# Values and keys in seven products each: keys' first product second, their fourth in front of the seventh, and VectorE's additions for the values ahead of the statistics

## The chip, the core and the metric

The kernel runs on one core of one Trainium2 chip. The metric is the device time of one execution in microseconds (us). The engines of the core are TensorE (PE; PEld is its loading of weights), VectorE (DVE), ScalarE (ACT), GpSimd (POOL) and SyncE (SP, which here only issues DMAs). A measurement of this kernel can tell a difference from none at about 0.2%, that is 4.7 us.

## The reference

Sixteen graphs of 1024 nodes with 256 features go through two layers. Everything is float32.

```python
# layer 0
h = relu(layernorm(x))
c = mean(h over features)                       # one number per node
A = 2 * abs(abs(sigmoid(c[None] - c[:, None]) - 0.5) - 0.5)
g = relu((h.T @ (adj * A)) * para)              # queries, [features, nodes]
k, v = split(h @ kv_w)                          # keys and values, 4 heads of 64
x = x + softmax(q @ k.T * scale) @ v            # attention over the 1024 nodes
# layer 1
h = relu(layernorm(x))
agg = A_hat @ h                                 # A_hat from adj, the same for all graphs
z = agg @ W1.T + b1;  z = relu(batchnorm(z));  z = z @ W2.T + b2
x = x + batchnorm(z)
```

Both batch norms go over all graphs, so there is a first long stage (layer 0, and layer 1 up to `z`) and a second stage that starts when all `z` are known.

## The kernel before

**The loop over graphs.** In the first stage the graphs `b` follow each other. In one pass TensorE does the attention of graph `b` (`attention`), then the queries, values and keys of graph `b + 1` (`graph_seven`), then layer 1 of graph `b` (`linear1`, `linear1_seven`). `graph_seven` runs in 14 passes. In 13 of them `linear1` follows it at once; in the last one (`last` is true) the attention of graph 15 follows, and layer 1 of graph 14 comes later. The order on every engine is written out by hand: inside `tc.manual_schedule` each engine executes in the order of the Python calls. Waits between engines are put in by the framework, from the tiles that instructions read and write.

**Seven products.** A matrix product of 2 by 2 blocks is done with seven block products in place of eight. The class `Seven` does it for the values (`V`, `turned`, so that nodes lie on partitions) and for the keys (`K`). Product 1 is written to one PSUM bank, `x`. ScalarE copies it out (`copy`, L728); then product 6 is added into the same bank, which is copied out again; then product 5, and product 3. Products 2, 7 and 4 have banks of their own, and VectorE adds them onto what was copied (`add`, L731). So a product that is added into `x` must wait until ScalarE has copied what stands there. One product is 8 matmul records of 128 columns for the values (L718) and 2 of 512 for the keys (L713).

**PSUM.** There are three buffers with the tag "s" (two banks each), one with "o" and one with "t". Values' `x` and fourth product and keys' `x` and seventh product take "s"; values' seventh and keys' fourth take "o", one after the other; both second products take "t". The two running sums of the queries, `gps`, hold two "s" buffers before that, and the first two tiles that come after (aggregation in `linear1`, or scores in the last pass) take the buffers of values' fourth product and keys' `x`.

**What stands around it on the other engines.** ScalarE copies the last sum of the queries (L656). VectorE makes sums of parts of `h` for the seven products (L663 to L667), finishes the queries (L657 to L670, L740), adds the attention's second half to `x` (`add1`, L938), and then takes the layer norm of this `x` (`norm`, with the class `Norm`) in two halves of four chunks. For each half: `stats` (L253 and L255) on VectorE, `invert` with the variance on VectorE (L259) and the power on GpSimd (`rstd`, L260), `shifts` on VectorE (L266, which waits for GpSimd), and `relu` on ScalarE (L281), one instruction a chunk, which writes `f_h_b`. The aggregation's first product (`f_aps`, L1027) reads `f_h_b` as weights, chunk by chunk, first the four chunks of the first half, then the second half's.

**SP.** The DMA queue of SP holds here, in order: `leave`, the store of `x` (L1279); `arrive`, the load of the `x` of a later graph into the same buffer (L191, 1 MB), which must wait until the last ReLU has read that buffer; two loads `f_t` (L998) and the load `f_w1s` (L1116). VectorE takes statistics of the arrived `x` (`f_st_a`, L253), GpSimd its power (L260), VectorE its shift (L266, behind the addition L1076 on its engine), and ScalarE its ReLU (`f_h_a`, eight chunks). Behind these on ScalarE stands the copy L1079 of the aggregation's running sum, into which the last product of the aggregation (`s4` by `resident(1, 1)`) is then added.

Of the kernel before, what the change touches and what calls it, by code (L numbers as in the profile page):

```python
# [29 lines left out]
def fast_path(  # L30
# [24 lines left out]
    NC = N // P  # L55
# [120 lines left out]
    with ExitStack() as stage:  # L176
# [332 lines left out]
        def graph_seven(b, left, norm, load_more, last):  # L509
# [224 lines left out]
            K = Seven("k", 0, lambda i, j: kT[:, i, ts(j, 512)], False)  # L734
            V.product(1)
            V.copy(0, 0)
            V.product(2)
            V.add(0, 0, 2)
            for d in range(CC):
# [1 line left out]
            V.product(7)  # L741
            V.product(6)
            V.copy(1, 0)
            K.product(1)
            K.copy(0, 0)
            add1()
            leave(b - 1)
            arrive(b + 1)
            load_more(2, 3)
            norm.stats(0, 4)  # L750
            norm.invert(0, 4)
            K.product(2)
            V.product(5)
            V.copy(1, 1)
            V.add(1, 0, 7)
            V.add(1, 1, 7)
            norm.shifts(0, 4)
            if last:
                K.add(0, 0, 2)
            norm.stats(4, NC)  # L760
            norm.invert(4, NC)
            K.product(6)
            K.copy(1, 0)
            V.product(4)
            V.add(1, 0, 4)
            V.product(3)
            V.copy(0, 1)
            todo = [lambda d=d: relu_queries(d) for d in range(CC)]
# [6 lines left out]
                relu_queries(1)  # L775
            else:
                norm.relu(0, 4, False)
            K.product(7)
            norm.shifts(4, NC)
            if not last:  # L780
                K.add(0, 0, 2)
            K.product(4)
            K.product(3)
            K.copy(0, 1)
            if not last:
# [596 lines left out]
        with tc.manual_schedule(engines={ENG.PE, ENG.Activation, ENG.DVE, ENG.Pool, ENG.SP}):  # L1382
# [3 lines left out]
            norm = Norm(xs[0], "a0", sums_of[0])  # L1386
# [69 lines left out]
            for b in range(B):  # L1456
# [25 lines left out]
                norm = Norm(xr[b], f"b{b}")  # L1482
# [17 lines left out]
                if b + 1 < B:  # L1500
                    more_loads = {}

                    def load_more(k0, k1):
                        if 0 < b < B - 2:
                            more_loads.update(load_thirds(b, k0, k1))

                    if b == 0:
                        qkv = graph(b + 1, between)
                        todo = []
                    else:  # L1510
                        qkv, todo = graph_seven(b + 1, left, norm, load_more, b + 2 == B)
                        thirds = more_loads
                    if b == 0:
                        for step in scale[4:]:
                            step()
                        thirds = make_thirds(b)
# [945 lines left out]
```

## Time and profile before

| | |
|---|---|
| Time, median of 4 runs | 2369.65 us (2369.29 to 2370.03) |
| The profiled execution | 2371.92 us, of which the span of its instructions is 2370.1 us |
| Granted TensorE clock, mean | 0.996 |
| Busy: TensorE, VectorE, ScalarE, GpSimd | 98%, 84%, 60%, 19% |
| From one pass to the next | about 129.2 us |
| Values and keys of one pass, up to the aggregation | 12.5 us |

A row of the timeline tells: start in us, duration in us, engine, line of the kernel, operation, what it writes from what it reads, shape, count of merged instructions; in brackets the engine's idle time ahead of it and what ended it. Matmul records overlap in the pipeline, so the distance of two starts says more than a duration. A weight load normally starts when the matmul before its own starts; its engine's "idle" in between costs nothing.

### The profile page before, as it was taken

The page shows a single profiled execution, that of the slowest core. Times are in us where ns is not written, and L with a number is a line of the kernel's source. Part 1 is how long each engine was busy: PE and PEld are TensorE (multiplying, and loading weights), DVE is VectorE, ACT ScalarE, POOL GpSimd, SP SyncE. Part 2 cuts the span into 40 slices and gives each one's busy share as a digit, 9 for nine tenths or more (in the row PEclk, how much of TensorE's full clock was granted, in tenths as well). Part 3 has the DMA queues.
Part 4 walks back from the last instruction along what each step waited for, and adds up shares of the span by engine and source line. Part 5 has one row for each costly group of instructions (what it writes and reads, how often), then busy time and mean ns, then how long its engine had stood idle before and what let it go on. Part 6 is the DMA issues. An engine that isn't in the chain of part 4 may idle for free.

```text
span 2370.1 us, 25709 instructions
## 1 busy us (share of the span) xinstructions
PE 2328.4 (98%) x8258; PEld 1034.0 (44%) x8258; DVE 1986.2 (84%) x2923; ACT 1417.4 (60%) x2057; POOL 441.9 (19%) x565
## 2 busy tenths in 40 slices
PE   8999999999999999999999999999999999999995
PEld 4444444434343434444343434344444434444444
DVE  6788989897989889897989798988989898757766
ACT  6846556574837465665657384746556575346654
POOL 2041212122221112221212221221212121100000
PEclk9999999999999999999999999999999999999998
DMA  5043343523342434334343324253353521355569
GB/s 187 18 137 104 133 142 116 158 109 116 118 142 78 169 98 155 121 126 150 109 132 132 126 81 159 89 178 98 133 142 116 158 73 54 130 213 179 175 235 375
DMA packets 167264, 323.78 MB, mean 137 GB/s; under 512 B 33616, under 2 KB 100688, under 8 KB 167120
## 3 DMA queue, kind: packets, MB, share of 16 engines
q1 hardware_dynamic: 143696, 266.44, 32.7%
q0 software_dynamic: 18816, 38.83, 6.0%
q10 hardware_dynamic: 4608, 16.78, 1.8%
q8 instruction: 67, 1.10, 0.2%
q14 instruction: 77, 0.63, 0.1%
HBM read 202.38 MB, written 100.72 MB: 128 GB/s over the span
## 4 chain that ended last, share of the span: by engine, by line
PE 93%; DMA 2%; DVE 2%; POOL 1%; issue 1%; ACT 0%; SPq 0%; DVEq 0%; ACTq 0%; POOLq 0%
PE f_s L810 19%; PE f_o L862 19%; PE f_aps L1027 16%; PE f_gps L571 8%; PE f_gpsx L571 6%; PE f_zps L1134 6%; PE f_zx L1684 4%; PE f_zm L1684 3%; PE f_vpsx L718 2%; PE f_kpsx L713 2%; PE f_vps L718 1%; PE f_kps L713 1%; PE f_gps L413 1%; DMA f_z<-fx 1%; PE f_vps L459 1%
## 5 line engine op out<-in xcount | busy, mean ns | idle before, releaser
L818 ACT ACTIVATE f_p<-f_s 128x1024 f32<-128x1024 f32 x512 | 477.0, 1044 | 60.7 <-PE f_s L810 60.6
L810 PE MATMUL f_s<-f_qT,f_kT 64*128 64x512 f32 x2048 | 457.0, 596 | 0.4 <-DVE f_v L731 0.4
L862 PE MATMUL f_o<-f_p,f_v 128*64 128x512 f32 x2048 | 453.6, 595 | 0.0
L810 PEld LDWEIGHTS f_s<-f_qT,f_kT 64*128 64x128 f32 x2048 | 191.1, 185 | 263.8 <-issue 116.9
L862 PEld LDWEIGHTS f_o<-f_p,f_v 128*64 128x64 f32 x2048 | 141.4, 137 | 304.3 <-issue 265.6
L366 POOL TENSOR_TENSOR f_w<-f_w,f_adj 128x1024 f32<-128x1024 f32 x56 | 132.5, 2366 | 701.5 <-ACT f_w L365 528.7
L930 POOL DMA_DIRECT2D f_att<-f_oT x256 | 136.7, 541 | 381.5 <-DVE f_oT L913 375.1
L833 DVE TENSOR_TENSOR f_acc<-f_acc,f_p 128x1024 f32<-128x1024 f32 x128 | 155.9, 1218 | 4.6 <-ACT f_p L818 4.6
L833 DVE TENSOR_TENSOR f_sums<-f_sums,f_p 128x1024 f32<-128x1024 f32 x128 | 155.8, 1217 | 0.0
L353 ACT ACTIVATE f_w<-f_row,f_col 128x1024 f32<-128x1024 f32 x127 | 147.5, 1161 | 7.2 <-DMA f_row<-frow 5.2
L356 ACT ACTIVATE f_w<-f_w 128x1024 f32<-128x1024 f32 x127 | 134.4, 1058 | 4.0
L1027 PE MATMUL f_aps<-f_ahatT,f_hs 128*128 128x512 f32 x256 | 115.1, 592 | 0.0
L1027 PE MATMUL f_aps<-f_ahatT,f_h_b 128*128 128x512 f32 x256 | 113.7, 597 | 0.3 <-DVE f_v L731 0.2
L365 ACT ACTIVATE f_w<-f_w,f_now 128x1024 f32<-128x1024 f32 x56 | 64.4, 1149 | 82.5 <-DVE f_now L363 82.5
L1027 PE MATMUL f_aps<-f_t,f_hs 128*128 128x512 f32 x256 | 112.5, 592 | 0.0
L571 PE MATMUL f_gps<-f_w,f_h_a 128*128 128x512 f32 x224 | 109.9, 592 | 0.0
L824 DVE TENSOR_TENSOR f_acc<-f_p,f_p 128x1024 f32<-128x1024 f32 x64 | 78.0, 1218 | 32.3 <-ACT f_p L818 32.3
L281 ACT ACTIVATE f_h_a<-f_x,f_shift_a,f_rstd_a 128x256 f32<-128x256 f32 x126 | 73.8, 587 | 38.2 <-DVE f_shift_a L266 38.2
L830 DVE TENSOR_TENSOR f_sums<-f_p,f_p 128x1024 f32<-128x1024 f32 x64 | 78.1, 1221 | 21.0 <-ACT f_p L818 21.0
L370 DVE SCALAR_TENSOR_TENSOR f_w<-f_w,f_adj 128x1024 f32<-128x1024 f32 x71 | 88.0, 1258 | 7.7 <-ACT f_w L356 7.6
L1157 ACT ACTIVATE f_z<-f_zps,f_b 128x512 f32<-128x512 f32 x60 | 38.0, 684 | 75.2 <-PE f_zps L1134 75.2
L846 DVE STREAM_TRANSPOSE f_sums<-f_acc 128x1024 f32<-128x1024 f32 x64 | 79.7, 1246 | 1.7
(298 smaller groups left out, 3964.9 us busy)
## 6 DMA issues: line engine op xcount, KB each, us to landing
f_t<-ft SPq DMA_DIRECT2D x84, 512.0 KB, 9.8
fz<-f_z SPq DMA_DIRECT2D x64, 512.0 KB, 9.6
f_x<-in_x_dram SPq DMA_DIRECT2D x31, 1024.0 KB, 6.0
f_zb<-fz SPq DMA_DIRECT2D x42, 512.0 KB, 4.3
fx<-f_x SPq DMA_DIRECT2D x16, 1024.0 KB, 4.4
fgs<-f_gs POOLq DMA_DIRECT2D x28, 512.0 KB, 3.0
fhT<-f_hQ POOLq DMA_DIRECT2D x112, 128.0 KB, 3.2
f_hT<-fhT SPq DMA_DIRECT2D x28, 512.0 KB, 6.2
```

The costliest lines, as they stand in the source:

```text
L353: nc.scalar.activation(w, rows[b], AF.Abs, bias=cols[b][:, c : c + 1], scale=0.5 / C)
L356: nc.scalar.activation(w, w, AF.Tanh)
L366: nc.gpsimd.tensor_mul(w, w, adj_t[c])
L571: nc.tensor.matmul(ps, left, right, start=fresh and n == 0, stop=(n == PAIRS - 1), skip_group_check=more,)
L810: nc.tensor.matmul(ps[:, e, :], kT[rows_e, pair, ts(m, P)], qT[rows_e, pair, ts(g, 512)], start=True, stop=True,)
L818: nc.scalar.activation(p, ps, AF.Exp)
L833: nc.vector.tensor_add(to, to, p)
L862: nc.tensor.matmul(o_of[s][e * HD : (e + 1) * HD, :], v[:, m, ts(2 * pair + e, HD)], p[:, e, :], start=(m == 0), stop=(m == NC - 1),)
L930: queue.dma_start(t[ts(j, 32), :, a].rearrange("r h c i -> r h (c i)"), oT[ts(a, 32), :, j].rearrange("r h c i -> r h (c i)"),)
L1027: nc.tensor.matmul(ps, left[:, m, :], right(m), start=not more and m == 0, stop=(m == KH - 1), skip_group_check=more,)
L1134: nc.tensor.matmul(ps[i], left[:, ts(i, P)], right, start=not more, stop=True, skip_group_check=more,)
L1684: nc.tensor.matmul(ps, left[:, m, :], right[:, m, :], start=start and m == 0, stop=(m == 1), skip_group_check=not start,)
```

## The change

No instruction is added or taken away. On TensorE two products move. Keys' first product moves from the fifth place to the second, directly behind values' first; keys' fourth moves ahead of keys' seventh. On VectorE the two additions of values' seventh product (`V.add(1, 0, 7)`, `V.add(1, 1, 7)`) now stand ahead of the first half's statistics, and the addition of values' fourth product ahead of the first half's shift and the second half's statistics, where it stood behind these. ScalarE, GpSimd and SP keep their order.

On TensorE the order was V1 V2 V7 V6 K1 K2 V5 K6 V4 V3 K5 K7 K4 K3 and becomes V1 K1 V2 V7 V6 K2 V5 K6 V4 V3 K5 K4 K7 K3 (V and K for values and keys, with the number of the product).

```diff
             V.product(1)
             V.copy(0, 0)
+            K.product(1)
             V.product(2)
             V.add(0, 0, 2)
             for d in range(CC):
                 nc.vector.tensor_mul(qT[:, d, :], both(d), qT[:, d, :])
             V.product(7)
             V.product(6)
             V.copy(1, 0)
-            K.product(1)
             K.copy(0, 0)
             add1()
             leave(b - 1)
             arrive(b + 1)
             load_more(2, 3)
-            norm.stats(0, 4)
-            norm.invert(0, 4)
             K.product(2)
             V.product(5)
             V.copy(1, 1)
             V.add(1, 0, 7)
             V.add(1, 1, 7)
-            norm.shifts(0, 4)
+            norm.stats(0, 4)
+            norm.invert(0, 4)
             if last:
                 K.add(0, 0, 2)
-            norm.stats(4, NC)
-            norm.invert(4, NC)
             K.product(6)
             K.copy(1, 0)
             V.product(4)
             V.add(1, 0, 4)
+            norm.shifts(0, 4)
+            norm.stats(4, NC)
+            norm.invert(4, NC)
             V.product(3)
             V.copy(0, 1)
...
-            K.product(7)
+            K.product(4)
             norm.shifts(4, NC)
             if not last:
                 K.add(0, 0, 2)
-            K.product(4)
+            K.product(7)
             K.product(3)
             K.copy(0, 1)
```

## The prediction

> **What bounds the kernel.** I read the page first (engine shares, chain), then the timeline of one pass of `graph_seven`, TensorE alone and then all engines, then the wait lists.
>
> ```profile
> PE 2328.4 (98%) x8258; PEld 1034.0 (44%) x8258; DVE 1986.2 (84%) x2923; ACT 1417.4 (60%) x2057; POOL 441.9 (19%) x565
> PE 93%; DMA 2%; DVE 2%; POOL 1%; issue 1%; ACT 0%; SPq 0%; DVEq 0%; ACTq 0%; POOLq 0%
> ```
>
> TensorE is busy 98% of the span and carries 93% of the chain, at a granted clock of 0.996. So only what moves TensorE's starts counts. The change touches 14 passes of about 129 us; in each, 14 products of values and keys run from 411.09 to 423.57 us (second pass, used below):
>
> ```profile
> 411.09 1.05 PE L718 MATMUL f_vpsx<-f_kvw,f_hT 128*128 128x128 f32 x8
> 411.98 1.11 PE L718 MATMUL f_vps<-f_kvw,f_hT 128*128 128x128 f32 x8
> 412.93 1.06 PE L718 MATMUL f_vps<-f_kvs,f_kt 128*128 128x128 f32 x8
> ...
> 419.97 1.02 PE L713 MATMUL f_kpsx<-f_hT,f_kvs 128*128 128x512 f32 x2
> 420.83 1.10 PE L713 MATMUL f_kps<-f_kt,f_kvs 128*128 128x512 f32 x2
> 421.77 1.02 PE L713 MATMUL f_kps<-f_kt,f_kvw 128*128 128x512 f32 x2
> 422.63 1.02 PE L713 MATMUL f_kpsx<-f_hT,f_kvs 128*128 128x512 f32 x2
> 423.57 7.11 PE L1027 MATMUL f_aps<-f_ahatT,f_h_b 128*128 128x512 f32 x16
> ```
>
> See the distances of starts: 0.89 for a product of values, 0.86 for one of keys, and three exceptions of 0.94-0.95: values' second, keys' seventh, keys' third. No idle is printed, but each stands at a late weight load:
>
> ```profile
> 411.93 0.97 PEld L718 LDWEIGHTS f_vps<-f_kvw,f_hT 128*128 128x128 f32 x8
> 420.81 0.30 PEld L713 LDWEIGHTS f_kps<-f_kt,f_kvs 128*128 128x128 f32 x2 [0.64 <-ACT f_v L728]
> 423.54 0.30 PEld L1027 LDWEIGHTS f_aps<-f_ahatT,f_h_b 128*128 128x128 f32 x2 [0.72 <-ACT f_h_b L281]
> ```
>
> Normally weights load while the matmul before runs. A late load at W starts the product's second half at W+0.53 (next loads at 421.34 and 424.07) instead of 0.43 after its due start M, so the cost is W-(M-0.10). That gives 0.05 at values' second (it waits for the copy L656, over at 411.88), 0.08 at keys' seventh (M 420.83) and 0.15 at the first aggregation (M 423.49; it waits for VectorE's addition of values' fourth, over at 423.42, whose PSUM buffer it takes). Together 0.28-0.29 us a pass.
>
> **The change, part by part.** No instruction is added or removed; POOL and SP issue the same lists.
>
> *TensorE order.* Keys' first between values' first and second delays the latter by 0.86: L656 is then long done, -0.05. Keys' first waits for the addition L658, over by 408.6: free. Keys' fourth waits for values' seventh's additions (forecast end 419.3, due 420.8): free. Behind it, keys' seventh finds its copy done: -0.08. The aggregation no longer waits for that late addition: -0.15, if its other wait (ReLU, below) holds. New: between values' sixth and fifth only one product is left instead of two. Sixth starts 414.63, ends 1.06 later at 415.69, its copy (0.59) ends 416.31, weights 416.36 (copy to weights took 0.05 in the rows above), M 416.39: +0.08. It is the case of keys' seventh at another place, since that also had one product of keys between. All products after it are behind it on TensorE. Sum to the aggregation: -0.20 (bounds: -0.29 if that copy is hidden, -0.12 if it costs twice).
>
> *VectorE order.* Values' second ends 0.86 later, so its addition starts at 414.01 instead of 413.77; all after it is 0.24 late. The two additions of values' seventh (0.60 each) now precede the first statistics: 1.20 more. Variance then stands at 420.92 instead of 419.49, GpSimd's rstd 421.24-422.27, the shift 422.31 instead of 420.87, with the addition of values' fourth under rstd (free: VectorE stands idle there). Behind the shift stand the second statistics, so all of this adds up. ReLU of the first four chunks: 422.52 instead of 421.51. Its first chunk (0.60) is done at 423.12, weights 423.17, needed by 423.33: free by 0.16. Later chunks come every 0.49 for 0.86 of matmul: free. Second half: shift 425.39 instead of 423.95, ReLU done 427.68 instead of 426.24, against a need at about 426.8 for its first chunk (ready 426.2): free. So the chain is 1.43 late, and this ends where nothing in the diff points:
>
> ```profile
> 426.27 0.39 SPq L191 DMA_DIRECT2D f_x<-in_x_dram  x1
> 432.00 2.71 DVE L253 BATCH_NORM_STATS2 f_st_a<-f_x 128x6 f32<-128x256 f32 x8 [0.53 <-DMA f_x<-in_x_dram]
> 435.60 1.64 POOL L260 TENSOR_TENSOR f_rstd_a<-f_var_a,f_mhalf 128x8 f32<-128x8 f32 x1 [11.68 <-DVE f_var_a L259]
> 438.25 0.16 DVE L266 SCALAR_TENSOR_TENSOR f_shift_a<-f_mv_a,f_rstd_a 128x8 f32<-128x8 f32 x1
> 443.13 0.56 ACT L1079 COPY f_u<-f_aps 128x512 f32<-128x512 f32 x1
> 444.24 3.60 PE L1027 MATMUL f_aps<-f_ahatT,f_hs 128*128 128x512 f32 x8
> ```
>
> *The SP queue.* The load of the next x writes the buffer that this ReLU reads; it issues 0.03 after the last chunk. It moves to 427.69 and, at 5.7 us to use (432.00-426.27), the statistics start at 433.42. Then by the rows: 3.29 to the variance, 0.31 and 1.64 for rstd, 0.04, 0.20 to ReLU, 4.68 of ReLU, L1079 0.56: its end moves from 443.69 to 444.14. Before, rstd was done at 437.24 and the shift had to stand behind the addition of 437.65, so 1.0 of the 1.43 is absorbed. TensorE's last aggregation product accumulates where L1079 reads: weights 444.19, M 444.24-0.20 = 444.04, needed 443.94: +0.25. The load takes longer on average (the statistics of the other passes start up to 0.3 later after their issue): I take +0.30. Bounds: 0 (load 0.3 faster) and +0.6 (all as slow as the slowest). Behind that load SP holds two f_t loads and f_w1s; 1.43 later they land at about 438 at most, for products at 440.8 and 451. The store of x goes 0.24 later, with 4 us to spare. GpSimd's DMAs of sums and turned h leave 0.5 later and are read a pass later. VectorE's own later work has its 2.19 idle before L1076; the row for the next tanh waits on its own DMA and no wait of TensorE on it is listed.
>
> The three late loads above cost 0.05 to 0.15 each, although the matmul before was still running. The Trainium skill, page "TensorE: Matmul & The Clock Gate", section "Architectural detail: the array is 16× 32×32, not 1× 128×128", says that TensorE's queue can pull weight loads ahead of matmuls in flight. Taken to hold for a load whose own operand or bank is still awaited, it would make every term of this kind zero and leave the last pass alone: 2370.5, an estimate. I go by the rows.
>
> *The last pass* has no ReLU there; scores follow:
>
> ```profile
> 1973.87 0.68 DVE L731 TENSOR_TENSOR f_v<-f_v,f_vps 128x512 f32<-128x512 f32 x1
> 1975.08 0.16 DVE L266 SCALAR_TENSOR_TENSOR f_shift_b<-f_mv_b,f_rstd_b 128x4 f32<-128x4 f32 x1 [0.53 <-POOL f_rstd_b L260]
> 1975.16 1.88 DVE L731 TENSOR_TENSOR f_kT<-f_kT,f_kps 128x512 f32<-128x512 f32 x3
> 1974.60 7.31 PE L810 MATMUL f_s<-f_qT,f_kT 64*128 64x512 f32 x32 [0.43 <-DVE f_v L731]
> ```
>
> The first score waited for values' fourth's addition (0.6 late in all); that goes. But the third takes the PSUM buffer of keys' seventh and waits for the second of the three additions, which follow the second shift: 0.24 + 1.20 later, less the 0.60 of values' fourth that the earlier rstd now covers: +0.85. The first gain lies inside this, so the pass costs +0.85 (bounds 0 and +1.4).
>
> **Sum.** 13 x (-0.20 + 0.30) + 0.85 = +2.15 us on a span of 2370.1. That execution took 2371.92; the runs' median is 2369.65, to which I add it: **2371.8**. A measurement of this kernel tells about 0.2% (4.7 us) from no change.
>
> **Rivals.**
> - *The x load stays hidden.* For it: only 0.25 is missing, and one pass's load comes 0.1 sooner. Against: the issue is bound to the ReLU. 13 x -0.20 + 0.85: 2367.9. The Trainium skill, page "DMA: Bandwidth & Descriptors", section "Anatomy of one DMA — SWDGE (gpsimd) path", fits 2.0 us plus bytes at 436 GB/s, for loads that GpSimd issues; by it this load would take 4.4 us, an estimate, and stay hidden; the row has 5.7.
> - *The chain to that load is longer than my rows, and it decides (slower).* Each 0.1 more goes to L1079 in full, above 0.16 at the first ReLU too. One pass already had rstd 0.29 late (its first aggregation starts 0.29 late). With 0.30 a pass: 2371.8 + 3.9 = 2375.7; beyond 0.2% from 0.2 more a pass.
> - *A plain gain.* Load hidden, values' fifth not late, last pass not hurt: 13 x -0.29 = -3.8, less 0.6 for the last: 2365.3. Against it speak three rows at once.
>
> **Numbers.** Forecast's case 0.55 (2370 to 2374), load hidden 0.2, chain longer 0.17, plain gain 0.08. Range 2367.0 to 2376.0. Faster by over 0.2%: the plain gain's lower half, 0.04. Slower: most of the longer chain, 0.14. Within: 0.82.
>
> **What would show it.** Values' second 0.89 before the next, values' fifth about 0.97, keys' seventh 0.86; `f_x` issued 1.4 us later after the pass's start; the last aggregation product late behind ACT L1079; in the last pass a wait of the third score on the keys' additions. I am wrong if the load lands early, or ReLU holds the first aggregation.

## The result, and the profile after

| | before | after |
|---|---|---|
| Time, median | 2369.92 us (52 runs, 2368.99 to 2371.66) | 2372.8 us (32 runs, 2371.28 to 2374.84) |
| Ratio | 1 | 1.0013, 95% interval 1.0008 to 1.0018 |
| The profiled execution | 2371.92 us, span 2370.1 us | 2373.37 us, span 2371.6 us |
| Granted TensorE clock | 0.996 | 0.997 |
| Thirteen passes, from values' first product of the first to that of the last | 1679.70 us (129.21 each) | 1682.73 us (129.44 each) |
| Last pass, to the second step of its scores | 27.25 us | 28.08 us |

The changed kernel is slower by 2.9 us (1.9 to 4.3 by the interval), against 2.15 forecast: within the 0.2% that counts as no difference, and inside the forecast's own case of 2370 to 2374 us.

The page of after, its engine shares and the shares of the chain that ended last:

```profile
PE 2328.2 (98%) x8258; PEld 1031.6 (43%) x8258; DVE 1986.7 (84%) x2923; ACT 1415.8 (60%) x2057; POOL 441.9 (19%) x565
PE 83%; DVE 6%; DMA 4%; ACT 3%; POOL 2%; issue 2%; DVEq 0%; ACTq 0%; SPq 0%; POOLq 0%
```

TensorE's busy time is as before, 98%. But it carries 83% of the chain where it carried 93%. DMA went from 2% to 4% and ScalarE from 0% to 3%: the chain now runs off TensorE and back through a load. The busy shares show nothing of this.

The timeline of the second pass, TensorE's matmuls, from values' first product to the aggregation (the same stretch as was shown of before):

```profile
411.56 1.05 PE L718 MATMUL f_vpsx<-f_kvw,f_hT 128*128 128x128 f32 x8
412.45 1.02 PE L713 MATMUL f_kpsx<-f_hT,f_kvw 128*128 128x512 f32 x2
413.31 1.05 PE L718 MATMUL f_vps<-f_kvw,f_hT 128*128 128x128 f32 x8
414.20 1.06 PE L718 MATMUL f_vps<-f_kvs,f_kt 128*128 128x128 f32 x8
415.09 1.06 PE L718 MATMUL f_vpsx<-f_kvs,f_kt 128*128 128x128 f32 x8
415.98 1.02 PE L713 MATMUL f_kps<-f_hT,f_kvw 128*128 128x512 f32 x2
416.85 1.14 PE L718 MATMUL f_vpsx<-f_kvs,f_hT 128*128 128x128 f32 x8
417.82 1.02 PE L713 MATMUL f_kpsx<-f_kt,f_kvs 128*128 128x512 f32 x2
...
421.32 1.02 PE L713 MATMUL f_kps<-f_kt,f_kvw 128*128 128x512 f32 x2
422.18 1.02 PE L713 MATMUL f_kps<-f_kt,f_kvs 128*128 128x512 f32 x2
423.04 1.02 PE L713 MATMUL f_kpsx<-f_hT,f_kvs 128*128 128x512 f32 x2
423.90 7.03 PE L1027 MATMUL f_aps<-f_ahatT,f_h_b 128*128 128x512 f32 x16
```

Take the distances of the starts. Values' second is followed after 0.89 us (was 0.94), keys' seventh after 0.86 (was 0.94), keys' third after 0.86 (was 0.94). One distance is new: values' fifth, 416.85 to 417.82, is 0.97. From values' first product to the aggregation this makes 12.34 us in place of 12.48. The timeline's rows of weight loads show the cause of the new one:

```profile
416.82 0.97 PEld L718 LDWEIGHTS f_vpsx<-f_kvs,f_hT 128*128 128x128 f32 x8 [0.64 <-ACT f_v L728]
```

This load waited for the copy of values' sixth product, while its matmul was due at 415.98 + 0.86 = 416.84. By the forecast's rule, load minus (due start minus 0.10), that is 0.08 us, and 0.08 is what the distance grew by. In all passes but the eleventh the aggregation's next product (`f_aps` from `f_t` and `f_hs`) starts 0.21 us earlier than before, 19.21 against 19.42 us after the pass's start.

Then the loss. The timeline of the same pass, all engines, along the path of the next `x`:

```profile
428.15 0.39 SPq L191 DMA_DIRECT2D f_x<-in_x_dram  x1
434.02 2.71 DVE L253 BATCH_NORM_STATS2 f_st_a<-f_x 128x6 f32<-128x256 f32 x8 [0.84 <-DMA f_x<-in_x_dram]
437.62 1.64 POOL L260 TENSOR_TENSOR f_rstd_a<-f_var_a,f_mhalf 128x8 f32<-128x8 f32 x1 [11.80 <-DVE f_var_a L259]
439.29 0.17 DVE L266 SCALAR_TENSOR_TENSOR f_shift_a<-f_mv_a,f_rstd_a 128x8 f32<-128x8 f32 x1 [0.70 <-POOL f_rstd_a L260]
444.18 0.56 ACT L1079 COPY f_u<-f_aps 128x512 f32<-128x512 f32 x1
444.79 0.30 PEld L1027 LDWEIGHTS f_aps<-f_ahatT,f_hs 128*128 128x128 f32 x2 [0.96 <-ACT f_u L1079]
```

Counted from the pass's start (411.56), the load of `x` is issued at 16.59 us (was 15.18). The shift of the next layer norm waits for GpSimd (before, it stood behind L1076). The copy L1079 stands behind all eight ReLU of that norm and ends at 33.19 (was 32.60). The last product of the aggregation, due at 32.94, waits for it. How that looks over all passes is in the list of groups, weight loads of this line and operands; the last column is idle time, and after each arrow what ended it and for how long in all. Before:

```profile
L1027 PEld LDWEIGHTS f_aps<-f_ahatT,f_hs 128*128 128x128 f32 x256 | 48.6, 190 | 61.2 <-issue 57.9 <-ACT f_u L1079 3.3
```

After:

```profile
L1027 PEld LDWEIGHTS f_aps<-f_ahatT,f_hs 128*128 128x128 f32 x256 | 47.6, 190 | 67.8 <-issue 54.8 <-ACT f_u L1079 13.0
```

An idle time of 0.24 us ahead of a weight load is ordinary and costs nothing; the 3.3 us of before are 14 such. After, the same wait holds 13.0 us.

The last pass after, by the timeline: two rows of VectorE (the second shift, and behind it the three additions to the keys), then two of TensorE (the scores):

```profile
1978.85 0.16 DVE L266 SCALAR_TENSOR_TENSOR f_shift_b<-f_mv_b,f_rstd_b 128x4 f32<-128x4 f32 x1 [1.12 <-POOL f_rstd_b L260]
1978.93 1.88 DVE L731 TENSOR_TENSOR f_kT<-f_kT,f_kps 128x512 f32<-128x512 f32 x3
1976.99 1.99 PE L810 MATMUL f_s<-f_qT,f_kT 64*128 64x512 f32 x8
1980.27 5.42 PE L810 MATMUL f_s<-f_qT,f_kT 64*128 64x512 f32 x24 [1.29 <-DVE f_kT L731]
```

The first score comes 0.55 us earlier after the pass's start than before (12.44 against 12.99), but ahead of the third TensorE stands idle for 1.29 us, until two of the three additions to the keys are done, behind the second shift. The second step of the scores is 0.83 us later than before.

The gains and losses of the two traces add up to 3.03 + 0.83 = 3.9 us; the medians differ by 2.9, and their interval reaches to 4.3, so the two do not contradict each other. The spans of the two profiled executions differ by only 1.5 us (2371.6 against 2370.1). What is missing there is the end of the program: from the first matmul of L1902 to the end the execution of before took 66.7 us and that of after 64.4. It also varies without any change ahead of it: an experiment below, the early copy in the kernel before, runs its passes and the way from the last pass to L1902 exactly as before does, and still ended 2.1 us sooner. So one execution's span isn't compared below; passes are, and medians.

### The profile page after: what moved, and what is told of

The parts are those of the page before. It is cut to its first block, busy times and chain, and to the rows that moved or that the text cites. A ratio compares the mean times of both kernels' runs of the same rounds, so it can differ in the third digit from the quotient of the medians.

```text
span 2371.6 us, 25709 instructions
## 1 busy us (share of the span) xinstructions
PE 2328.2 (98%) x8258; PEld 1031.6 (43%) x8258; DVE 1986.7 (84%) x2923; ACT 1415.8 (60%) x2057; POOL 441.9 (19%) x565
## 4 chain that ended last, share of the span: by engine, by line
PE 83%; DVE 6%; DMA 4%; ACT 3%; POOL 2%; issue 2%; DVEq 0%; ACTq 0%; SPq 0%; POOLq 0%
PE f_s L810 19%; PE f_o L862 19%; PE f_aps L1027 9%; PE f_gps L571 8%; PE f_gpsx L571 6%; PE f_zps L1134 6%; PE f_zx L1684 4%; PE f_zm L1684 3%; DMA f_x<-in_x_dram 2%; ACT f_h_a L281 2%; DVE f_st_b L253 1%; DVE f_st_a L253 1%; POOL f_rstd_b L260 1%; PE f_gps L413 1%; PE f_vpsx L718 1%
## 5 line engine op out<-in xcount | busy, mean ns | idle before, releaser
L281 ACT ACTIVATE f_h_b<-f_x,f_shift_b,f_rstd_b 128x256 f32<-128x256 f32 x128 | 66.2, 591 | 37.1 <-DVE f_shift_b L266 37.1
```

Source lines behind the costliest of these rows:

```text
L281: nc.scalar.activation(self.h[:, c, :], self.xt[:, c, :], AF.Relu, bias=self.shift[:, c : c + 1], scale=self.rstd[:, c : c + 1], accum_out ...
```

## The experiments

Each experiment is compared with runs of the kernel before on the same chip (median 2370.10 us in 33 runs for copy early, the two orders alone and all mended; 2370.27 us in 27 for the other three). For each kernel the table has what its trace says against before's (thirteen passes, plus the last pass to the second step of its scores), and what the medians say.

| run | thirteen passes | last pass | sum by the trace | by the medians | ratio, 95% |
|---|---|---|---|---|---|
| after | +3.03 | +0.83 | +3.9 | +2.9 | 1.0008 to 1.0018 |
| copy early | -2.89 | +0.83 | -2.1 | -1.9 | 0.9983 to 1.0001 |
| TensorE order only | +3.12 | +0.23 | +3.4 | +3.4 | 1.0003 to 1.0022 |
| VectorE order only | -1.04 | +0.59 | -0.4 | -0.3 | 0.9993 to 1.0011 |
| all mended | -3.89 | -0.81 | -4.7 | -4.7 | 0.9969 to 0.9987 |
| sixth first | +1.39 | +0.84 | +2.2 | +3.0 | 1.0004 to 1.0022 |
| last pass | +1.79 | -0.73 | +1.1 | +2.1 | 1.0000 to 1.0018 |
| copy early, before | 0.00 | 0.00 | 0.0 | 0.0 | 0.9993 to 1.0011 |

### The kernel after, with the copy L1079 ahead of the last three ReLU

If the last aggregation product waits because the copy stands behind eight ReLU of a late `x`, then putting the copy after the fifth must bring the loss back, with nothing else touched.

```diff
+        def prepare_half(b):
+            norms[b].relu(0, NC // 2 + 1)
+            hs[b] = norms[b].h
+
+        def prepare_rest(b):
+            norms.pop(b).relu(NC // 2 + 1, NC)
...
             nc.scalar.copy(u3, sum_ps)
+            if len(between) > 3:
+                between[3]()
...
-                        lambda: (prepare_end(b + 2), pair_sums(b + 2, 0, 2)),
+                        lambda: (prepare_half(b + 2), pair_sums(b + 2, 0, 2)),
...
+                        rest=(lambda: prepare_rest(b + 2),),
```

> The changed kernel with one more move: ScalarE's copy of the aggregation's running sum (L1079) stands after five of the eight ReLU chunks of the next graph, not after all eight. Theory (the loss runs over the x load): in the changed kernel the load issues 1.42 us later after the pass's start (16.60 for 15.18), its statistics and ReLU follow late, and the last aggregation product waits for the copy behind them (third to last product distance 3.73 in the second pass where 3.43 is due). With three chunks of 0.585 fewer ahead of the copy, the copy ends about 1.7 earlier, at some 31.5 after the pass's start, and that product is due at 32.94: no wait, distance 3.43 in every pass. The products of values and keys keep their gain of 0.21 a pass, the last pass its loss of 0.84: 13 x -0.21 + 0.84 = -1.9 us against the kernel before, some 2368.0. Rival (the loss comes from VectorE's own later work, or from transfers in each other's way): the copy's place does not matter and the time stays near 2372.8.

Measured: 2368.22 us (2367.27 to 2370.37). Its timeline in the second pass, ScalarE and TensorE (the lines of the kernel are shifted by seven):

```profile
440.47 0.56 ACT L1086 COPY f_u<-f_aps 128x512 f32<-128x512 f32 x1
...
442.34 0.19 PEld L1034 LDWEIGHTS f_aps<-f_ahatT,f_hs 128*128 128x128 f32 x1 [0.24 <-ACT f_h_a L281]
442.76 3.60 PE L1034 MATMUL f_aps<-f_ahatT,f_hs 128*128 128x512 f32 x8
```

The load of `x` is as late as in after (16.59 us), and lands as late. But the copy is over at 441.03 and the weights of the last product load with the ordinary 0.24 us ahead of them. Eleven of the thirteen passes take 128.96 to 128.97 us, against 129.17 before: the -0.20 that was forecast up to the aggregation is kept to the end once nothing takes it away. So the loss of the thirteen passes is this one wait. The times agree: the ratio to before is 0.9983 to 1.0001 here and 1.0008 to 1.0018 in after, and the two intervals don't meet; that this version is faster than before, its interval doesn't show. By its trace the pass loses 0.42 us in after against this run (scores start 48.92 us after the pass's start on average, here 48.50).

### The early copy in the kernel before

The gain could have come from the early copy itself. The same edit in the kernel before:

> The kernel before with the early copy alone (the copy L1079 after five of the eight ReLU of the next x instead of behind all eight). My theory: in the kernel before, the last aggregation product is not held up by this copy, so there is nothing to win: 129.2 us from pass to pass and the same time as before, 2370.0 us (2369.5 to 2370.5). Rival (the early copy is worth something by itself, and the gain of the run with the kernel after and the early copy came from there): 13 x -0.3 to -0.4 = -4 to -5, about 2365.5 us.

Measured: 2370.23 us (2369.22 to 2371.96), and 1679.70 us for the thirteen passes, the same as before to the hundredth. Before, the copy was no bound; the change made it one.

### TensorE's order alone

After, with VectorE's order put back:

```diff
             load_more(2, 3)
+            norm.stats(0, 4)
+            norm.invert(0, 4)
             K.product(2)
...
-            norm.stats(0, 4)
-            norm.invert(0, 4)
+            norm.shifts(0, 4)
             if last:
                 K.add(0, 0, 2)
+            norm.stats(4, NC)
+            norm.invert(4, NC)
...
             V.add(1, 0, 4)
-            norm.shifts(0, 4)
-            norm.stats(4, NC)
-            norm.invert(4, NC)
```

> The kernel before with the moves on TensorE alone; VectorE keeps its old order. Theory (the two halves belong together): keys' fourth product needs the bank of values' seventh, whose second addition ends at 9.77 + 0.24 = 10.01 after the pass's start (0.24 because values' second product now comes later), so its weights load near 10.12 where 9.68 is needed: a wait of about 0.45. To the aggregation a pass changes by -0.05 (values' second) -0.08 (keys' seventh) +0.08 (values' fifth) -0.15 (the aggregation no longer waits, since all is later) +0.45 = +0.25; the x load is only 0.24 later and hidden. 13 x 0.25 + 0.25 in the last pass = +3.5 us: some 2373.4. Rival (TensorE's order is a gain by itself): -0.05 a pass, 2369.3 or less.

Measured: 2373.52 us (2371.93 to 2374.4). The timeline of TensorE, the weight load of keys' fourth, and VectorE's additions of values' seventh, second pass:

```profile
420.18 1.02 PE L713 MATMUL f_kpsx<-f_hT,f_kvs 128*128 128x512 f32 x2
421.41 1.10 PE L713 MATMUL f_kps<-f_kt,f_kvw 128*128 128x512 f32 x2 [0.20 <-DVE f_v L731]
...
421.38 0.30 PEld L713 LDWEIGHTS f_kps<-f_kt,f_kvw 128*128 128x128 f32 x2 [1.00 <-PE f_kpsx L713]
...
419.99 1.28 DVE L731 TENSOR_TENSOR f_v<-f_v,f_vps 128x512 f32<-128x512 f32 x2
```

Keys' fourth takes the PSUM buffer of values' seventh, and the two additions that free it end at 421.27 when they stand behind the statistics. So the product, due at 421.04, has its weights at 421.38: 0.44 us. Every pass loses 0.24 us on balance. TensorE's order needs VectorE's.

### VectorE's order alone

After, with TensorE's order put back:

```diff
             V.copy(0, 0)
-            K.product(1)
             V.product(2)
...
             V.copy(1, 0)
+            K.product(1)
             K.copy(0, 0)
...
-            K.product(4)
+            K.product(7)
             norm.shifts(4, NC)
...
-            K.product(7)
+            K.product(4)
```

> The kernel before with the moves on VectorE alone; TensorE keeps its old order. Theory: values' second and keys' seventh stay late (0.05, 0.08), values' fifth is on time, the aggregation starts on time (-0.15). The x load issues 1.20 later (two additions of 0.60), so the copy L1079 ends at about 33.0 after the pass's start and the last aggregation product, due at 33.00, waits about 0.2: about +0.05 a pass, and +0.6 in the last pass (its second shift comes 0.6 later). 13 x 0.05 + 0.6 = +1.2 us: some 2371.1. Rival (VectorE's order is a gain because it ends the late start of the aggregation, 13 x -0.15 = -2.0, and the last pass's first score, -0.6): 2367.4.

Measured: 2369.84 us (2368.96 to 2372.81), 1.3 us under what I expected, and by its interval not to be told from before. The last pass loses 0.59 us. But in the thirteen passes I had counted the wait for L1079 each time, and here the load of `x` is issued at 16.35 us, 0.24 earlier than in after. Its group row of the weight loads:

```profile
L1027 PEld LDWEIGHTS f_aps<-f_ahatT,f_hs 128*128 128x128 f32 x256 | 47.9, 190 | 63.3 <-issue 54.8 <-ACT f_u L1079 8.2
```

8.2 us, between the 3.3 of before and the 13.0 of after. In eight passes the next graph's scores start 48.54 to 48.58 us after the pass's start, the copy being in time or nearly so; in five they start at 48.66 to 48.93. The wait isn't a fixed price but the part of a spread that hangs over an edge.

### Values' sixth ahead of their seventh

The 0.08 us at values' fifth can be had back by a second product between the sixth and the fifth:

```diff
-            V.product(7)
             V.product(6)
             V.copy(1, 0)
+            V.product(7)
             K.copy(0, 0)
```

> The kernel after with one more edit: on TensorE the values' sixth product and its copy stand ahead of the values' seventh, so that two products lie between the sixth and the fifth again. My theory: the fifth's distance falls from 0.97 to 0.89 us and the first aggregation product comes about 0.08 us earlier (12.344 to about 12.26 after the pass's start), but the last aggregation product does not: it waits for the copy L1079, whose time is set by the load of x and not by TensorE. So from pass to pass 129.4 us as before the edit, wait there 0.08 larger, and the time stays at 2372.8 us (2372.3 to 2373.2). Rival: what TensorE gains at the front it keeps to the end: 13 x -0.08 = -1.0, 2371.8 us.

Measured: 2373.29 us (2371.61 to 2374.78); theory and rival lie 1 us apart, less than this interval, so the trace has to tell them apart. The timeline of TensorE in the second pass (its start is at 412.40), and the last product's weights:

```profile
417.69 1.05 PE L718 MATMUL f_vpsx<-f_kvs,f_hT 128*128 128x128 f32 x8
418.58 1.02 PE L713 MATMUL f_kpsx<-f_kt,f_kvs 128*128 128x512 f32 x2
...
445.49 3.70 PE L1027 MATMUL f_aps<-f_ahatT,f_hs 128*128 128x512 f32 x8
...
445.49 0.30 PEld L1027 LDWEIGHTS f_aps<-f_ahatT,f_hs 128*128 128x128 f32 x2 [0.90 <-ACT f_u L1079]
```

Values' fifth is down to 0.89 and the aggregation starts 12.26 us after the pass's start, 0.08 earlier than in after. But the last product starts on average 10.78 us after the start of the statistics of the loaded `x`, in this run as in after (33.18 - 22.40 and 33.27 - 22.49). It is tied to the load, not to TensorE. Its passes are 0.13 us shorter than after's because the statistics of the loaded `x` start 0.09 earlier (the loads of this execution were quicker), and because one pass of after lost 0.4 elsewhere (below), which is 0.03 on average; the 0.08 that was won went into the wait.

### The last pass

```diff
             norm.shifts(0, 4)
-            norm.stats(4, NC)
-            norm.invert(4, NC)
+            if not last:
+                norm.stats(4, NC)
+                norm.invert(4, NC)
...
-            norm.shifts(4, NC)
             if not last:
+                norm.shifts(4, NC)
                 K.add(0, 0, 2)
...
                 late()
+                norm.stats(4, NC)
+                norm.invert(4, NC)
+                norm.shifts(4, NC)
```

> The kernel after with one more edit, in the last pass alone: there the additions to the keys stand ahead of the second half's statistics and shift on VectorE. My theory (the third score's wait is for the second of these additions, behind the second statistics): the second step of the scores of that pass starts 1.2 to 1.4 us earlier than in the kernel after (28.08 to about 26.8 after the pass's start), the 1.29 us of idle ahead of the third score goes, and the time is 2371.4 us. The thirteen other passes stay at their 129.4 us. Rival (the wait belongs to something else, or comes back at the late shift): 2372.8 us.

Measured: 2372.37 us (2370.38 to 2374.06). The timeline of TensorE and VectorE in its last pass (the scores' line is shifted by four):

```profile
1974.69 7.14 PE L814 MATMUL f_s<-f_qT,f_kT 64*128 64x512 f32 x32
1981.76 7.09 PE L866 MATMUL f_o<-f_p,f_v 128*64 128x512 f32 x32
...
1973.94 1.88 DVE L731 TENSOR_TENSOR f_kT<-f_kT,f_kps 128x512 f32<-128x512 f32 x3 [0.30 <-PE f_kps L713]
1975.74 1.40 DVE L253 BATCH_NORM_STATS2 f_st_b<-f_x 128x6 f32<-128x256 f32 x4
```

The scores run as one stretch without idle, and the second step starts 26.52 us after the pass's start, 1.56 earlier than in after and 0.73 earlier than before. That settles whom the third score waited for. By the medians the loss against before is 2.1 us in place of 2.9, a gain of 0.8 where 1.4 was expected; the interval holds theory and rival, so the time doesn't tell.

### All three mended

The early copy, values' sixth first and the last pass's order together, on top of the change:

> The changed kernel with three more moves: the copy L1079 after five ReLU chunks (as in the first run); values' sixth product ahead of the seventh, so that two products stand between sixth and fifth; and in the last pass the three late additions of the keys ahead of the second statistics. Theory: each undoes one of the three losses. To the aggregation -0.29 a pass (values' second, keys' seventh, aggregation), no wait at the last product, and in the last pass no wait of the first and third score (about -0.65 against before). 13 x -0.29 - 0.65 = -4.4 us against before: some 2365.5. Rival (the waits hide each other, or another one stands right behind): not below the first run's time.

Measured: 2365.38 us (2363.49 to 2366.8): 4.7 us under before, ratio 0.9978 (0.9969 to 0.9987), and 7.4 us under after (2372.8). All distances in its passes are 0.86 or 0.89. Its group row (lines shifted by eleven) names L1079's copy no more:

```profile
L1038 PEld LDWEIGHTS f_aps<-f_ahatT,f_hs 128*128 128x128 f32 x256 | 48.6, 190 | 61.2 <-issue 59.8 <-ACT f_h_a L281 1.4
```

Eleven passes take 128.88 us: here values' sixth ahead of the seventh is worth its 0.08 to 0.09 us a pass against the run with the early copy alone, which it wasn't in after. By the intervals this version lies under both kernels; the 4.7 us against before are just the 0.2% that a measurement of this kernel can tell from none.

## Why the prediction was right

**Up to the aggregation: as forecast.** The terms were -0.05 (values' second), -0.08 (keys' seventh), -0.15 (the aggregation) and +0.08 (values' fifth), -0.20 in sum. The distances show each, 0.97 at values' fifth included; of the aggregation's 0.15 they show 0.08, and the rest, which lay inside that product, shows at the next one. There the sum is -0.21. The ReLU of the first half was to be free by 0.16: the weights of the first aggregation product are loaded at 423.62, due 423.90 less 0.10, free by 0.18.

**The chain on VectorE and SP: as forecast.** The first shift was to come 1.43 later, the load of `x` 1.43: measured from the pass's start, shift 9.78 to 11.22, load 15.18 to 16.60.

**The wait at the last aggregation product: right in its place, too small.** Forecast +0.30 on average, measured +0.42. The mis-sized term is the load. Its issue came where it was forecast (16.60 us after the pass's start), and from the start of the statistics to the end of L1079 it is 10.72 to 10.73 us in each of the thirteen passes, as the terms of the forecast add up to (444.14 - 433.42). Between the two the forecast had 5.73 us from the second pass and 0.05 more for the others, which is near the average of before (5.80). In after the average is 5.87, with landings from 5.52 to 6.21 us after the issue, and the eleventh pass issues 0.29 later than the rest; together that is the missing 0.1. The average is not steady from execution to execution: in the seven experiments it lies between 5.75 and 5.90. So a part of the difference between forecast and result is the luck of an execution's loads. The estimate from the Trainium skill, page "DMA: Bandwidth & Descriptors", section "Anatomy of one DMA — SWDGE (gpsimd) path", of 4.4 us for such a load was further off than the row (5.7, measured 5.87 on average); that section speaks of loads that GpSimd issues, and no run here shows one of this size.

**The last pass: as forecast.** +0.85 against +0.83, by the wait that was named: the third score for the second of the keys' additions.

**Sum.** Scores start 0.20 us later after the pass's start on average (48.92 against 48.72): 13 x 0.20 + 0.83 = 3.4. The trace's 3.9 contains, besides, one pass of after in which the third step of the scores came 0.4 us late behind a late load (`f_row`). The medians' 2.9 lies between this and the forecast's 2.15.

**The rivals.** The hidden load fell with the first run (2368.22 only once the copy no longer stood behind the ReLU). The longer chain to the load did not come: the load is issued at 16.60 us as forecast. What was longer was the load itself, which that rival did not name, and it cost 0.12 a pass in place of 0.30. The plain gain of 2365.3 did not come from the change; the run with all three mended came to that time once each of the three rows held against it had been taken away.

**Late weights.** The forecast priced a load of weights that waits for its operand or its bank by the rows. It did not price it at zero, as one could by the Trainium skill, page "TensorE: Matmul & The Clock Gate", section "Architectural detail: the array is 16× 32×32, not 1× 128×128", which says that TensorE's queue can pull weight loads ahead of matmuls in flight, if one takes that to hold for awaited loads too. The runs agree with the rows: 0.08 at values' fifth, 0.44 at keys' fourth with TensorE's order alone, 0.42 on average at the last aggregation product. Only the first is a test of it: there the matmul ahead still ran (by its row to 417.00) when the load started at 416.82. In the other two it had just ended.

## What to carry to other kernels

A step moved later on an engine off the critical path takes its DMAs along: here 1.4 us on VectorE became 1.4 us on the load that reuses the buffer, and came back on TensorE some 25 us behind the edit, through a copy that only stood in line behind that load's ReLU. So follow a moved step through the buffer it frees, the load into it, and everything queued behind that load's readers; the cure was to move the copy in its queue, not to undo the change. And price a wait that hangs on a DMA by its landings in all passes, not by one row: with VectorE's order alone the early ones won nothing and the late ones cost in full.

## What the runs showed that was not expected

- A saving ahead of a wait is no saving: values' sixth ahead of the seventh was worth nothing by the trace while the last product hung on the load, and about 0.08 us a pass with the copy early.
- The eleventh pass in every run has its power on GpSimd some 0.29 us later than the others. Before it costs the first aggregation product 0.29 us; in after, where that product waits for the ReLU with 0.18 to spare, it costs 0.01 and 0.10 at the second half. Why that pass, no run shows.
- The end of the program, from the first matmul of L1902 on, took 64.4 and 66.7 us in the profiled executions of after and before, and with the schedule of before unchanged it moved by 2.1 us. Differences of the size studied here are read from the passes first.
